# Attention kernel on one core: the weighted sum of values turned around, stationary values in four column groups

## The chip, the cores and the metric

The kernel runs on one core of a Trainium2 chip. The metric is device time in microseconds from launch to end. All arithmetic on data is in f32; the logits use f32r, a form of f32 that TensorE takes in one pass.

## The reference

Two layers, each `x + f(groupnorm(x))`, on an image of 48 channels and 256 x 256 pixels. Layer 0, where the change lies, is attention over patches:

```python
qkv = jnp.einsum('bchw,oc->bohw', x, w_qkv)         # 144 channels
qkv = dwconv3x3(qkv, w_dw)                          # depthwise 3x3
q, k, v = jnp.split(qkv, 3, axis=1)
q, k, v = (heads(q), heads(k), heads(v))            # unfold 4x4 patches with a border of 4: 8 heads, 96 features, 66*66 tokens
q = _l2norm(q); k = _l2norm(k)                      # over the 96 features of a token
attn = jnp.einsum('bhcn,bhcm->bhnm', q, k) * temperature
attn = jax.nn.softmax(attn, axis=-1)                # over m
out = jnp.einsum('bhcn,bhnm->bhcm', v, attn)        # sum over n
out = fold(out.reshape(b, -1, out.shape[-1]), h, w)
out = jnp.einsum('bchw,oc->bohw', out, w_proj)
```

The tokens of the border are zero: their logits are zero, so they only add a constant to each softmax denominator. 4096 tokens of the image remain. Layer 1 multiplies 64 x 64 windows by three sets of matrices along width, height and channels.

## The kernel before, in words

**Stages.** Loading x and its statistics; the pointwise product for heads 0 and 1; the depthwise stage of head 0; attention over eight heads; the projection with the residual and the statistics for layer 1; layer 1. In the profile attention runs from about 288 to 3240 us.

**Attention.** The loop runs over 8 heads, and in each over 16 steps `g` of two blocks of 128 query tokens. The order is written out by hand (`tc.manual_schedule`): each engine gets its instructions in the order of the code. In one step:

- `scores` makes the logits of a block of 128 tokens against all 4096: four times six matmuls (L339) into a PSUM tile of two banks called `big` (three buffers), each followed by an exponential on ScalarE (L574) which writes `e` and its sum. A step makes two such blocks, the second one being the first of the next step.
- `normalised` adds the four sums on VectorE (L587), adds the border's part from a table `e0` made once (L589, `e0` at L563), takes the reciprocal (L591) and scales the block's values with it into `vn` (L593), 128 tokens x 96 features.
- `weigh` makes the weighted sum for all 4096 tokens, in four rounds k. The stationary operand is a piece of `e` of 128 x 64, the moving one is `vn` with 96 columns; two such pieces fill the two column halves of the array. Each round fills 768 columns of a `big` tile (L603), tokens on partitions. VectorE copies it (L612, first step of a head) or adds it (L614) to the sum `oacc` in SBUF.
- Between these, VectorE, ScalarE and POOL do the depthwise convolution of the next head, one row of patches per step in steps 0 to 11: nine taps (L211, L230), squares (L241), their sum (L245), a small matmul `norm` that adds over partitions (L249, `pn`), the inverse square root by three Newton steps on VectorE (`root`, L253 to L270), scaling (L276) and copies and stores to DRAM (L281, L287, L291, L297). The taps of row g-1 and the root of row g-2 are in the same step.
- Head 0 also carries the pointwise product of the other six heads, as strips (L179, L182) between the rounds of `weigh`, in `big` tiles as well.

At the end of a head the sums have tokens on partitions and must have features there. `store` does that for 512 tokens at a time: four transposes on TensorE (L620, `pt` in the PSUM pool `one`), a copy on ScalarE (L623, `oo`) and two DMAs on POOL's queue (L625) to the DRAM tensor `os_`. They are placed behind rounds 1 to 3 of the last step, and the last two in the first step of the next head. POOL's queue also holds the load of key 7 of the next head, ahead of them. SP's queue loads keys, queries, values and rows.

**Behind attention.** The projection loads `os_` (L782, `pot`) in 16 tiles, in pairs: tile t of the upper half of the image and of the lower. A matmul (L796), an addition (L803) and statistics (L807) follow.

Of the kernel before, what the change touches and what calls it, by code (L numbers as in the profile page):

```python
# [1 line left out]

# [6 lines left out]
F32 = mybir.dt.float32  # L9
F32R = mybir.dt.float32r  # L10
AF = mybir.ActivationFunctionType
ALU = mybir.AluOpType
# [10 lines left out]
NH = 8  # L23
HD = C * KK // NH
NT = (H // KS) * (W // KS)
NBORDER = (H // KS + 2) * (W // KS + 2) - NT
# [5 lines left out]
NP1 = CH * HC  # L32
# [7 lines left out]
TP = 256  # L40
# [5 lines left out]
def conv_preact_kernel(  # L46
# [15 lines left out]
    nc = tc.nc  # L62
# [60 lines left out]

    nmul = const.tile([NP1, NH], F32, name="nmul")
    nadd = const.tile([NP1, 1], F32, name="nadd")

    def group_stats(st, mean, rstd, pool, pspool, behind=lambda: None):

# [35 lines left out]
    class Strip:  # L164
# [24 lines left out]
        def store(self):  # L189
            for s, rows in enumerate(both_halves(t1[1], 2 * self.j, 2, base=1)):  # L190
                nc.sync.dma_start(out=rows, in_=self.ot[:, 2 * s : 2 * s + 2, :])

    class Depthwise:
# [57 lines left out]
        def root(self, on_scalar=False):  # L251
            n = self.pool.tile([NP1, PX], F32, name="n", bufs=2)
            nc.vector.tensor_scalar_max(n, self.pn, 1e-24)  # L253
            y = self.pool.tile([NP1, PX], F32, name="y", bufs=2)
            if on_scalar:
                nc.scalar.activation(n, n, AF.Sqrt)
                nc.vector.reciprocal(y, n)
                nc.vector.tensor_scalar(y, y, nmul[:, self.h : self.h + 1], nadd, ALU.mult, ALU.add)
                self.y = y
                return  # L260

            nc.vector.tensor_scalar(
                y.bitcast(mybir.dt.int32), n.bitcast(mybir.dt.int32), -0.5, 1597463007.0, ALU.mult, ALU.add
            )
# [38 lines left out]
    NB = NT // 128  # L303
# [101 lines left out]
    with tc.tile_pool(name="xn", bufs=1) as xnp, tc.tile_pool(name="cst", bufs=1) as cst, tc.tile_pool(  # L405
# [124 lines left out]
    with tc.tile_pool(name="ahead", bufs=2) as ah, tc.tile_pool(name="ae", bufs=3) as ae, tc.tile_pool(  # L530
        name="asm", bufs=6
    ) as asm, tc.tile_pool(name="ao", bufs=1) as ao, tc.tile_pool(name="big", bufs=3, space=PSUM) as big:
        MB = 8
        NK = NB // MB
        NLATE = 1
        RP = TP // PX * KS
        NG = NB // G
        keys, queries, values, oaccs = {}, {}, {}, {}
# [26 lines left out]
        def scores(h, nb):  # L565
# [15 lines left out]
            return h, nb, e, zs  # L581

        def normalised(h, nb, e, zs):

            b = h * NB + nb
# [5 lines left out]
            nc.vector.reciprocal(rz, zu)  # L591
# [4 lines left out]
        def weigh(h, g, blocks, k):  # L596

            ps = big.tile([128, 2, 512], F32, name="big")
            for j in range(MB):
                mb = k * MB + j  # L600
                for i, (e, vn) in enumerate(blocks):
                    for p in (0, 64):
                        nc.tensor.matmul(  # L603
                            ps[p : p + 64, j // 4, j % 4 * HD : (j % 4 + 1) * HD],
                            lhsT=e[:, mb * 128 + p : mb * 128 + p + 64],
                            rhs=vn,
                            start=(i == 0),
                            stop=(i == G - 1),
                        )
            if g == 0:  # L610
                oaccs[h, k] = ao.tile([128, 2, 4 * HD], F32, name="oacc", bufs=5)
                nc.vector.tensor_copy(oaccs[h, k], ps[:, :, : 4 * HD])  # L612
            else:
                nc.vector.tensor_add(oaccs[h, k], ps[:, :, : 4 * HD], oaccs[h, k])  # L614

        def store(h, m):

            pt = one.tile([HD, 4, 128], F32, name="pt", tag="one")
            for i in range(4):
                nc.tensor.transpose(pt[:, i, :], oaccs[h, m // 2][:, m % 2, i * HD : (i + 1) * HD], ident)  # L620
            late = h == NH - 1 and m >= NM - NLATE
            oo = (pe if late else asm).tile([HD, 512], F32, name="oo", bufs=NLATE if late else 2)
            nc.scalar.copy(oo, pt.rearrange("p i n -> p (i n)"))  # L623
            for i in range(512 // TP):
                nc.gpsimd.dma_start(  # L625
                    out=os_[m * (512 // TP) + i, h * HD : (h + 1) * HD, :], in_=oo[:, i * TP : (i + 1) * TP]
                )

        load_query(0, 0)
        for m in range(NM):  # L630
# [13 lines left out]
        with tc.manual_schedule():  # L644
            load_query(0, 1)
            block = scores(0, 0)
            for h in range(NH):
                more = h + 1 < NH
                rows = {r: Depthwise(h + 1, r) for r in range(CR + 1)} if more else {}
                for g in range(NG):  # L650
# [51 lines left out]
                    if g == 0 and h > 0:  # L702
                        for m in range(6, 8):
                            store(h - 1, m)
                    if p:
                        p.patches()
                        p.store((2,))
# [4 lines left out]
                        n.first()  # L712
                    for k in range(NK):
                        s = (h * NG + g) * NK + k
                        weigh(h, g, blocks, k)
                        if k == 0 and d:
                            d.reduce()
                        if k == 0 and p:
                            p.low(nc.gpsimd)
                            p.store((0, 1))  # L720
                        if s % 2:
                            for w in strips[s - 1] + strips[s]:
                                w.run(big.tile([128, 2, 512], F32, name="big"))
# [20 lines left out]
            for m in range(6, 8):  # L744
                store(NH - 1, m)
    attention.close()


# [307 lines left out]
```

## Time and profile before

| | |
|---|---|
| runs | 3646.11, 3650.18, 3638.68 us; median 3646.11 |
| the profiled execution | 3654.33 us, its span 3652.5 us |
| mean granted TensorE clock | 0.974 |
| attention: PE L339, L603 | 6144 and 32768 MATMUL instructions |
| ScalarE L574 | 1024 x 1117 ns, and 1024 x 192 ns to read the sums |
| VectorE L614 | 480 x 954 ns |
| PE L620 and ScalarE L623 | 256 x 277 ns and 64 x 582 ns |

The page gives busy time per engine and the chain of work that ended last. Busy time of PE counts the union of its matmuls, which overlap, so single durations do not add up to it; a price per matmul is read from a stretch of the timeline, as its length over its count. An f32 matmul of the program appears as two MATMUL instructions, an f32r one as one. The span is what the profile covers; the execution's own time is 1.8 us more.

### The profile page before, as it was taken

What the parts mean: (1) busy time and instruction counts of PE and PEld (TensorE: products, weight loads), DVE (VectorE), ACT (ScalarE), POOL (GpSimd) and SP (SyncE); (2) the same over time, 40 slices, a digit from 0 to 9 for tenths busy, and PEclk for the clock granted to TensorE, in tenths of its full rate; (3) what the DMA queues carried; (4) which work ended last, traced back from release to release, by engine and by line L of the source; (5) the groups of instructions that cost most, each with busy time, mean ns of one, the idle gap of its engine ahead of it and who ended that gap; (6) DMA issues with size and microseconds to landing.
All of it is one profiled execution on the core that took longest, in us unless ns stands there. A gap on an engine that the chain in (4) does not pass through costs nothing.

```text
span 3652.5 us, 104961 instructions
## 1 busy us (share of the span) xinstructions
PE 3426.0 (94%) x46578; PEld 2874.1 (79%) x46578; DVE 2115.9 (58%) x3505; ACT 1898.0 (52%) x2699; POOL 531.6 (15%) x616
## 2 busy tenths in 40 slices
PE   2878999999999999999999999999999999976888
PEld 1337777888888888889888888888889888842765
DVE  5464775269727962796289528952894222257454
ACT  0245666566646664665466546654665444410343
POOL 2030121012201220122112111211121100010001
PEclk9988999999999999999999999999999999987899
DMA  7455665533323332333233323332333221059564
GB/s 159 157 125 146 169 183 154 172 92 97 91 74 87 95 86 74 86 93 94 73 82 98 90 81 82 93 86 81 82 93 92 62 54 28 19 141 283 119 156 107
DMA packets 241972, 386.78 MB, mean 106 GB/s; under 512 B 78130, under 2 KB 175778, under 8 KB 237000
## 3 DMA queue, kind: packets, MB, share of 16 engines
q1 hardware_dynamic: 187974, 244.77, 24.0%
q0 software_dynamic: 35264, 106.40, 12.8%
q10 hardware_dynamic: 18274, 28.83, 3.4%
q8 instruction: 368, 6.03, 0.7%
q14 instruction: 92, 0.75, 0.1%
HBM read 234.76 MB, written 144.90 MB: 104 GB/s over the span
## 4 chain that ended last, share of the span: by engine, by line
PE 81%; DMA 4%; DVE 3%; issue 2%; ACT 1%; SPq 1%; ACTq 0%; POOL 0%; POOLq 0%; DVEq 0%
PE big L339 37%; PE big L603 36%; PE pc L961 2%; PE pb L942 2%; PE pa L916 2%; PE big L179 1%; DVE acc L230 1%; PE pt L620 1%; DMA pxt<-in_x_dram 1%; DMA pad<-t 1%; PE pn L249 1%; DMA xs<-in_x_dram 1%; PE pst L557 1%; DVE xt L803 1%; DVE lzt L928 0%
## 5 line engine op out<-in xcount | busy, mean ns | idle before, releaser
L574 ACT ACTIVATE e<-big,nmx 128x1024 f32<-128x1024 f32 x1024 | 1143.9, 1117 | 878.0 <-PE big L339 617.8
L339 PE MATMUL big<-kt,qt 128*128 128x512 f32 x6144 | 1439.9, 393 | 31.9 <-DMA qt<-qkv 21.7
L603 PEld LDWEIGHTS big<-vn,e 128*64 128x64 f32 x32768 | 1358.7, 137 | 57.1 <-ACT e L574 30.6
L603 PE MATMUL big<-vn,e 128*64 128x96 f32 x32768 | 1389.1, 247 | 5.9 <-DVE oacc L614 2.4
L339 PEld LDWEIGHTS big<-kt,qt 128*128 128x128 f32 x6144 | 1148.4, 189 | 279.2 <-issue 29.3
L614 DVE TENSOR_TENSOR oacc<-big,oacc 128x768 f32<-128x768 f32 x480 | 453.4, 954 | 703.7 <-PE big L603 703.7
L230 DVE SCALAR_TENSOR_TENSOR acc<-pad,dwt,acc 126x1024 f32<-126x1024 f32 x592 | 765.6, 1293 | 39.7 <-ACT acc L211 23.9
L587 DVE TENSOR_REDUCE zt<-zs 128x1 f32<-128x4 f32 x256 | 38.5, 150 | 338.7 <-ACT e L574 338.7
L297 POOL DMA_DIRECT2D qkv<-o x72 | 52.8, 734 | 1247.6 <-ACT o L281 1247.6
L291 POOL TENSOR_TENSOR ol<-o,oh 126x1024 fp32r<-126x1024 f32 x78 | 184.7, 2368 | 311.7 <-DVE ss L245 238.4
L574 ACT ACTIVATION_READ_ACCUMULATOR e<-big,nmx 128x1 f32 x1024 | 196.2, 192 | 0.0
L281 ACT COPY o<-acc 126x1024 f32<-126x1024 f32 x74 | 158.8, 2146 | 0.0
L928 DVE COPY lzt<-pa 128x864 f32<-128x864 f32 (+1 forms) x69 | 101.2, 1507 | 69.2 <-PE pa L916 69.2
L949 ACT COPY lyt<-pb 128x1024 f32<-128x1024 f32 x69 | 70.7, 1025 | 116.3 <-PE pb L942 96.9
L241 ACT ACTIVATE sq<-acc 126x1024 f32<-126x1024 f32 x74 | 78.2, 1057 | 101.2 <-DVE acc L230 101.2
L796 PE MATMUL pps<-pot,wp 96*96 96x512 f32 x128 | 77.5, 770 | 56.2 <-DMA pot<-os__70 45.1
L182 ACT ACTIVATE ot<-big,bias 108x1024 f32<-108x1024 f32 x64 | 68.3, 1111 | 113.5 <-PE big L179 76.4
L211 ACT ACTIVATE acc<-pad,dwt 126x1024 f32<-126x1024 f32 x74 | 84.1, 1137 | 81.9 <-DMA pad<-t 81.9
L245 DVE TENSOR_REDUCE ss<-sq 126x64 f32<-126x1024 f32 x80 | 97.5, 1219 | 27.0 <-ACT sq L241 27.0
L942 PEld LDWEIGHTS pb<-wsb,lzt 64*64 64x64 f32 x4608 | 82.2, 140 | 37.2 <-issue 23.4
L219 PE MATMUL dps<-pad,diag 126*126 126x512 f32 x216 | 96.3, 606 | 15.5 <-DMA pad<-t 15.5
L796 PEld LDWEIGHTS pps<-pot,wp 96*96 96x96 f32 x128 | 26.0, 212 | 107.0 <-issue 73.8
(134 smaller groups left out, 2006.8 us busy)
## 6 DMA issues: line engine op xcount, KB each, us to landing
pad<-t SPq DMA_DIRECT2D x238, 254.0 KB
t<-ot SPq DMA_DIRECT2D x128, 217.7 KB
qkv<-ol POOLq DMA_DIRECT2D x78, 336.0 KB, 6.5
qkv<-oh POOLq DMA_DIRECT2D x70, 336.0 KB, 5.7
qt<-qkv SPq DMA_DIRECT2D x176, 96.0 KB
xs<-in_x_dram SPq DMA_DIRECT2D x128, 96.0 KB
os__70<-oo POOLq DMA_DIRECT2D x128, 96.0 KB, 2.1
pot<-os__70 SPq DMA_DIRECT2D x16, 768.0 KB
```

The lines of the kernel that those rows point to most:

```text
L219: nc.tensor.matmul(ps[:, i, :], lhsT=diag[:, tap, :], rhs=self.pad[:, y : y + 2, dx : dx + W], start=(tap == 0), stop=(tap == 8),)
L230: nc.vector.scalar_tensor_tensor(self.acc, self.pad[:, dy : dy + KS, dx : dx + W], dwt[:, self.h, tap : tap + 1], self.acc, ALU.mult, ALU.add,
L245: nc.vector.tensor_reduce(self.ss, self.sq.rearrange("p a (x b) -> p x a b", b=KS), AX.XY, ALU.add)
L281: nc.scalar.copy(self.o.rearrange("p (a b) x -> p a b x", a=KS), self.acc.rearrange("p a (x b) -> p a b x", b=KS))
L291: eng.tensor_sub(self.ol, self.o, self.oh.bitcast(F32))
L339: nc.tensor.matmul(ps[:, i, :], lhsT=qt[:, r, q0 : q0 + 128], rhs=kts[2 * j + i][:, r // 2, :], start=(r == 0), stop=(r == 2),)
L574: nc.scalar.activation(e[:, j * 1024 : (j + 1) * 1024], ps.rearrange("p a b -> p (a b)"), AF.Exp, bias=nmx[:, b : b + 1], accum_out=zs[:, ...
L603: nc.tensor.matmul(ps[p : p + 64, j // 4, j % 4 * HD : (j % 4 + 1) * HD], lhsT=e[:, mb * 128 + p : mb * 128 + p + 64], rhs=vn, start=(i == 0),
L614: nc.vector.tensor_add(oaccs[h, k], ps[:, :, : 4 * HD], oaccs[h, k])
L796: nc.tensor.matmul(ps[:, i : i + step, :], lhsT=wp, rhs=ot[:, ki * KS + i : ki * KS + i + step, part * n : (part + 1) * n], start=True, st ...
L928: nc.vector.tensor_copy(to, src)
L942: nc.tensor.matmul(pb[s * WS : (s + 1) * WS, w, n * WS : (n + 1) * WS], lhsT=zts[u][r, t * C + b * 24 + q * 8 + s * 4 + i, :], rhs=wsb[r, ...
```

## The change

`weigh` swaps its operands. The stationary operand is now a third of `vn`, 128 tokens x 32 features, and the moving one is 512 columns of `e`. Four such pieces stand side by side in four column groups of 32; each writes 32 partitions of a bank of a `big` tile, features on partitions. Three of the groups hold the three thirds for one set of 512 tokens, the fourth holds one third for the last set of four. So eight sets of 512 tokens fill six banks ("slots"), three `big` tiles a step in place of four. `store` then needs no transpose: four DMAs for each pair of slots go from `oacc` to `os_`, right behind the last addition. The fourth pass of the k loop keeps only the strips and loads that were attached to it. The last sum of all has a tile of its own (`last`).

The border's part of the denominator is an exponential with the bias log(NBORDER) into a fifth column of `zs`, at the head of every `scores`; `e0` and L589 go. The small matmul `norm` moves from ahead of `scores` to behind its first six logits. `root` takes one third-order step and one Newton step (seven operations for nine, ten in all), with a constant folded into `nmul3`.

```diff
-            for _ in range(3):
-                nc.vector.tensor_mul(z, y, y)
-                nc.vector.scalar_tensor_tensor(z, z, -0.5, n, ALU.mult, ALU.mult)
-                nc.vector.scalar_tensor_tensor(y, z, 1.5, y, ALU.add, ALU.mult)
-            nc.vector.tensor_scalar(y, y, nmul[:, self.h : self.h + 1], nadd, ALU.mult, ALU.add)
+            nc.vector.tensor_mul(z, y, y)
+            nc.vector.tensor_mul(z, z, n)
+            nc.vector.scalar_tensor_tensor(z, z, -10.0 / 3.0, z, ALU.add, ALU.mult)
+            nc.vector.scalar_tensor_tensor(y, z, 5.0, y, ALU.add, ALU.mult)
+            nc.vector.tensor_mul(z, y, y)
+            nc.vector.scalar_tensor_tensor(z, z, -0.5 * 0.375**2, n, ALU.mult, ALU.mult)
+            nc.vector.scalar_tensor_tensor(y, z, 1.5, y, ALU.add, ALU.mult)
+            nc.vector.tensor_scalar(y, y, nmul3[:, self.h : self.h + 1], nadd, ALU.mult, ALU.add)
...
+        nc.vector.tensor_scalar_mul(nmul3, nmul, 0.375)
...
-        e0 = ao.tile([128, NH * NB], F32, name="e0")
-        nc.scalar.activation(e0, nmx, AF.Exp)
+        border = ao.tile([128, 1], F32, name="border")
+        nc.vector.memset(border, math.log(NBORDER))
...
-            zs = asm.tile([128, 4], F32, name="zs")
+            zs = asm.tile([128, 5], F32, name="zs")
+            nc.scalar.activation(zs[:, 4:5], nmx[:, b : b + 1], AF.Exp, bias=border)
...
+                if j == 0 and behind:
+                    behind()
...
-            zu = asm.tile([128, 1], F32, name="zu")
-            nc.vector.scalar_tensor_tensor(zu, e0[:, b : b + 1], float(NBORDER), zt, ALU.mult, ALU.add)
...
+        def parts_of(slot):
+            q, j = divmod(slot, NS)
+            return q * (NS + 1) + j, q * (NS + 1) + NS, j
...
-            for j in range(MB):
-                mb = k * MB + j
+            for u in range(2):
+                m, last, j = parts_of(2 * pair + u)
                 for i, (e, vn) in enumerate(blocks):
-                    for p in (0, 64):
+                    for p in range(NS + 1):
+                        c, n = (p, m) if p < NS else (j, last)
                         nc.tensor.matmul(
-                            ps[p : p + 64, j // 4, j % 4 * HD : (j % 4 + 1) * HD],
-                            lhsT=e[:, mb * 128 + p : mb * 128 + p + 64],
-                            rhs=vn,
+                            ps[p * 32 : (p + 1) * 32, u, :],
+                            lhsT=vn[:, c * 32 : (c + 1) * 32],
+                            rhs=e[:, n * 512 : (n + 1) * 512],
                             start=(i == 0),
                             stop=(i == G - 1),
                         )
...
+            old = oaccs[h, pair]
+            if h == NH - 1 and g == NG - 1 and pair == 2:
+                oaccs[h, pair] = pe.tile([128, 2, 512], F32, name="last")
+            nc.vector.tensor_add(oaccs[h, pair], ps, old)
...
-            pt = one.tile([HD, 4, 128], F32, name="pt", tag="one")
-            for i in range(4):
-                nc.tensor.transpose(pt[:, i, :], oaccs[h, m // 2][:, m % 2, i * HD : (i + 1) * HD], ident)
...
-            nc.scalar.copy(oo, pt.rearrange("p i n -> p (i n)"))
...
+            for u in range(2):
+                m, last, j = parts_of(2 * pair + u)
+                for p0, p1, n, c in ((0, HD, m, 0), (HD, 128, last, j * 32)):
+                    rows = os_[n * T : (n + 1) * T, h * HD + c : h * HD + c + p1 - p0, :]
+                    nc.gpsimd.dma_start(
+                        out=rows.rearrange("t c n -> c t n"),
+                        in_=oaccs[h, pair][p0:p1, u, :].rearrange("c (t n) -> c t n", t=T),
+                    )
...
                     blocks = [normalised(*block)]
+                    block = scores(h, g * G + 1, p and p.norm)
                     if p:
-                        p.norm()
                         p.root()
-                    block = scores(h, g * G + 1)
...
-                        weigh(h, g, blocks, k)
+                        if k < 3:
+                            weigh(h, g, blocks, k)
+                            if g == NG - 1:
+                                store(h, k)
...
-                        if g == NG - 1 and k > 0:
-                            for m in range(2 * k - 2, 2 * k):
-                                store(h, m)
-            for m in range(6, 8):
-                store(NH - 1, m)
```

More of the change, by code (lines that the diff above doesn't have):

```diff
@@ L1 @@
+import math
 from contextlib import ExitStack
@@ L125, in conv_preact_kernel @@
     nadd = const.tile([NP1, 1], F32, name="nadd")
+    nmul3 = const.tile([NP1, NH], F32, name="nmul3")
     def group_stats(st, mean, rstd, pool, pspool, behind=lambda: None):
@@ L532, in conv_preact_kernel @@
     ) as asm, tc.tile_pool(name="ao", bufs=1) as ao, tc.tile_pool(name="big", bufs=3, space=PSUM) as big:
-        MB = 8
-        NK = NB // MB
-        NLATE = 1
+        NK = 4
+        NS = 3
         RP = TP // PX * KS
@@ L560, in turn, with scores @@
             values[h, m] = vT
-        e0 = ao.tile([128, NH * NB], F32, name="e0")
-        nc.scalar.activation(e0, nmx, AF.Exp)
-        def scores(h, nb):
+        border = ao.tile([128, 1], F32, name="border")
+        nc.vector.memset(border, math.log(NBORDER))
+        def scores(h, nb, behind=None):
             b = h * NB + nb
             e = ae.tile([128, NT], F32, name="e")
-            zs = asm.tile([128, 4], F32, name="zs")
+            zs = asm.tile([128, 5], F32, name="zs")
+            nc.scalar.activation(zs[:, 4:5], nmx[:, b : b + 1], AF.Exp, bias=border)
             kts = [keys[h, m] for m in range(NM)]
@@ L580, in scores @@
                 )
+                if j == 0 and behind:
+                    behind()
             return h, nb, e, zs
         def normalised(h, nb, e, zs):
-            b = h * NB + nb
             zt = asm.tile([128, 1], F32, name="zt")
             nc.vector.tensor_reduce(zt, zs, AX.X, ALU.add)
-            zu = asm.tile([128, 1], F32, name="zu")
-            nc.vector.scalar_tensor_tensor(zu, e0[:, b : b + 1], float(NBORDER), zt, ALU.mult, ALU.add)
             rz = asm.tile([128, 1], F32, name="rz")
-            nc.vector.reciprocal(rz, zu)
+            nc.vector.reciprocal(rz, zt)
             vn = asm.tile([128, HD], F32, name="vn")
@@ L594, in normalised, with weigh @@
             return e, vn
-        def weigh(h, g, blocks, k):
+        def parts_of(slot):
+            q, j = divmod(slot, NS)
+            return q * (NS + 1) + j, q * (NS + 1) + NS, j
+        def weigh(h, g, blocks, pair):
             ps = big.tile([128, 2, 512], F32, name="big")
-            for j in range(MB):
-                mb = k * MB + j
+            for u in range(2):
+                m, last, j = parts_of(2 * pair + u)
                 for i, (e, vn) in enumerate(blocks):
-                    for p in (0, 64):
+                    for p in range(NS + 1):
+                        c, n = (p, m) if p < NS else (j, last)
                         nc.tensor.matmul(
-                            ps[p : p + 64, j // 4, j % 4 * HD : (j % 4 + 1) * HD],
-                            lhsT=e[:, mb * 128 + p : mb * 128 + p + 64],
-                            rhs=vn,
+                            ps[p * 32 : (p + 1) * 32, u, :],
+                            lhsT=vn[:, c * 32 : (c + 1) * 32],
+                            rhs=e[:, n * 512 : (n + 1) * 512],
                             start=(i == 0),
@@ L610, in weigh, with store @@
             if g == 0:
[L611 to L616, printed above, removed]
-            pt = one.tile([HD, 4, 128], F32, name="pt", tag="one")
-            for i in range(4):
[L620 to L627, printed above, removed]
+                oaccs[h, pair] = ao.tile([128, 2, 512], F32, name="oacc", bufs=4)
+                nc.vector.tensor_copy(oaccs[h, pair], ps)
+                return
+            old = oaccs[h, pair]
+            if h == NH - 1 and g == NG - 1 and pair == 2:
+                oaccs[h, pair] = pe.tile([128, 2, 512], F32, name="last")
+            nc.vector.tensor_add(oaccs[h, pair], ps, old)
+        def store(h, pair):
+            T = 512 // TP
+            for u in range(2):
[6 more added lines that the diff above has]
+                    )
         load_query(0, 0)
@@ L701, in conv_preact_kernel @@
                             turn(h + 1, (g - CR - 2) * 2 + m)
-                    if g == 0 and h > 0:
-                        for m in range(6, 8):
-                            store(h - 1, m)
                     if p:
@@ L739, in conv_preact_kernel @@
                                 )
-                        if g == NG - 1 and k > 0:
-                            for m in range(2 * k - 2, 2 * k):
-                                store(h, m)
-            for m in range(6, 8):
-                store(NH - 1, m)
     attention.close()
```

## The prediction, made before the changed kernel was run

> **What bounds the kernel now.** I read the busy shares first, then the chain of waits, then three kinds of detail: the table of windows, the groups, and the timeline of one step.
>
> ```profile
> PE 3426.0 (94%) x46578; PEld 2874.1 (79%) x46578; DVE 2115.9 (58%) x3505; ACT 1898.0 (52%) x2699; POOL 531.6 (15%) x616
> ...
> PE big L339 37%; PE big L603 36%; PE pc L961 2%; PE pb L942 2%; PE pa L916 2%; PE big L179 1%; DVE acc L230 1%; PE pt L620 1%; DMA pxt<-in_x_dram 1%; DMA pad<-t 1%; PE pn L249 1%; DMA xs<-in_x_dram 1%; PE pst L557 1%; DVE xt L803 1%; DVE lzt L928 0%
> ```
>
> TensorE is busy 94% of the span, and the chain that ends last runs 73% through two lines: the logits (L339) and the weighted sum (L603). The table of windows (window, length, then busy us and instructions of PE, PEld, DVE, ACT, POOL, then clock, DMA share, GB/s) says where this is so:
>
> ```profile
> 306.00:745.00 439.00, 429.91 (x5230) 346.78 (x5229) 234.71 (x412) 282.53 (x383) 58.64 (x56) 0.99 0.58 163
> 1103.00:1461.00 358.00, 358.00 (x4951) 321.15 (x4949) 233.42 (x412) 213.35 (x313) 60.69 (x60) 1.00 0.34 86
> 3251.00:3380.00 129.00, 85.56 (x158) 31.10 (x158) 103.65 (x111) 0.41 (x2) 9.09 (x18) 0.74 0.98 272
> ```
>
> From head 1 on PE has no idle time at all: what comes off PE there comes off the span. Head 0 holds 9 us of gaps. The projection stage (3251 to 3380) is a DMA stage, 98% busy, so it moves earlier by as much as its first load does.
>
> The timeline (start, duration, engine, line, count) gives the price of a step, then of a head's boundary, then of the end of attention:
>
> ```profile
> 1505.18 10.78 PE L603 MATMUL big<-vn,e 128*64 128x96 f32 x256
> 1515.89 0.43 PE L249 MATMUL pn<-ss,same 126*126 126x64 f32 x2
> 1516.13 11.15 PE L339 MATMUL big<-kt,qt 128*128 128x512 f32 x48
> 1527.21 10.78 PE L603 MATMUL big<-vn,e 128*64 128x96 f32 x256
> ...
> 1798.90 1.08 PE L620 MATMUL pt<-ident,oacc 128*96 128x128 f32 x8
> 1799.91 2.86 PE L603 MATMUL big<-vn,e 128*64 128x96 f32 x64
> ```
> ```profile
> 3215.28 0.39 PE L603 MATMUL big<-vn,e 128*64 128x96 f32 x4
> ...
> 3237.21 2.03 POOL L625 DMA_DIRECT2D os__70<-oo  x4 [1.14 <-ACT oo L623]
> ...
> 3240.32 21.05 SPq L782 DMA_DIRECT2D pot<-os__70  x7
> ```
>
> A step is 22.03 us (1505.18 to 1527.21), a round of logits and a round of weighted sum of nearly equal length.
>
> **What the Trainium skill says.** "TensorEngine Tiling (Array Packing)", Tiling Modes, lists 128x32 with four tiles that work independently. The trace shows tiles working side by side: a plain f32 matmul of the program is two MATMUL instructions, and the 256 of a step pass in 10.78 us, 0.25 of it the last one's own length, so a pair passes in 10.53/127 = 83 ns. "TensorE: Matmul & The Clock Gate", Part 3, measured 10.6 times for a 4x4 packing of 32x32 tiles. There, four tiles share the same rows, as four column groups over 128 rows do; no line of this trace has more than two tiles on one row. "ScalarE: Activation LUTs", What ACT_TABLE_LOAD costs, gives an ACTIVATE with a pointer bias as 280 ns + 0.833 ns per element: 1133 ns for 1024, where L574 takes 1117.
>
> **The change part by part.**
>
> *Weighted sum on PE.* Before: 128 pairs x 83 ns = 10.6 us a step. After: 3 pairs of slots x 2 x 2 blocks x 4 groups = 48 program matmuls, 96 instructions of 512 columns. If four column groups run together that is 24 rounds. The nearest row is over_h (L961), four tiles of 64x64 (two on a row), also f32 with 512 columns:
>
> ```profile
> 3504.55 2.76 PE L961 MATMUL pc<-lyt,hsb 64*64 64x512 f32 x24
> ```
>
> 24 instructions are six rounds; less the last one's 0.59 (its shortest duration), five intervals take 2.17 us, 0.43 each. So 24 x 0.43 = 10.3 us, 0.3 less, and over 128 steps **-38 us**. The arithmetic that the array does has not shrunk (3 x 4096/4 columns a block against 32 x 96); only the overhead between rounds falls. Both ends: -38 if the four groups overlap fully, and a doubling of the 10.3 if only two do (rival 1).
>
> *Transposes.* Two stores before (8 transposes) put 1.01 us between parts of L603 (1798.90 to 1799.91). Four such pairs per head, 7 boundaries: **-28 us**. The oo copies (L623, 64 x 582 ns) go from ScalarE, where nothing waited at those places but the DMA. 128 store DMAs on POOL's queue at 0.51 us become 96 of the same kind, still behind the load of key 7 and before nothing else of that head; POOL is busy 15%.
>
> *End of attention.* Before, 25.0 us pass from the last step's first L603 (3215.28) to the first pot load (3240.32): the wait for vn, the rounds, then transposes, copies and DMAs in turn. After: resumed 2.1 us in, pairs of slots end at about 4.7, 8.1 and 11.5 us (3.44 each). The first loads need slots of the first two pairs only, and the last pair's sum has its own tile, so their buffers need not wait for it. 8.1 + 0.35 to release + up to 1.8 behind a memset (L760) + 1.23 add + 4 x 0.51 issue + 2.1 landing = 13.8 to 15.6: **-10 us** (-9 to -12). The DMA stage behind it then starts that much earlier.
>
> *Head 0.* The strips between the rounds want `big` buffers that wait for L614, because DVE is still at the taps. One buffer fewer a step and a shorter DVE queue: between 0 and the 9 us of gaps; I take **-4**.
>
> *VectorE, priced at nothing.* Per step: two root operations (2 x 226 ns), two zu (2 x 160) go; four additions of 768 columns at 954 become three of 1024, at the 1225 of L975 (same shape): 3.82 against 3.68. In a depthwise step DVE has some 21.2 us of work in 22.03, so it falls to about 20.2 in 21.7: PE stays the bound and covers it. Without cover, these would have been about 1 us a step. nmul3 is one small operation before attention.
>
> *ScalarE, priced at nothing.* 256 border exponentials, 202 ns (L145, 96x1) to 280 ns (skill) each, 52 to 72 us. The first of a step runs while ScalarE waits for logits (4.6 us there). The second is queued in front of an e, whose logits come every 1.36 us while an e costs 1.31; the lag of 0.2 is below the slack of three `big` buffers. If that cover failed, 72 us would appear. The e0 operation (0.4 us) goes.
>
> *Square sums' matmul moved (norm).* Same 0.2 us of PE, now after the first six logits, 1.4 us later. It issues no DMA. Behind it wait the other 42 logits; its own input was ready before the step. On DVE root follows the addition and normalised, which end 2.2 us into the step; pn is there at about 1.9. So nothing, with an upper end of 0.3 x 70 = 21 us.
>
> Sum: -38 - 28 - 10 - 4 = **-80 us**. Against the profiled execution (3654.3, span 3652.5) 3574; that execution lies 8 us above the median of the runs (3646.1), so for the median **3566 us**.
>
> **Rivals.** (1) *Four column groups over all 128 rows are not fed at full rate* (slower). For: only two tiles per row were ever seen here. Against: the 4x4 figure of the skill. If two pass at once, a round costs 0.86 and the step 10.0 us more: 3646 + 1280 - 42 = 4884. It decides from 80/3072 = 26 ns per round: at 457 ns instead of 430 the whole gain is gone. (2) *ScalarE or the moved matmul becomes visible*: +72, 3638, no measurable change. Against: ACT is 213 of 358 us busy. (3) *The rounds bring nothing* (lead-in of the 32-column groups eats 0.3 us a step), boundaries and end remain: 3604. That the transposes stay is excluded, the code that issues them is gone.
>
> **How the numbers follow.** My forecast 0.71; rival 3 0.10; rival 2 0.04; rival 1 0.15. Only differences above 0.3% (11 us) can be told from no change here. Faster 0.81, same 0.04, slower 0.15. The range takes the forecast with its ends (-38, -28, -12, -9, and 21 back) and rival 3, from 3540 to 3630; rival 1 is left out.
>
> **What would show it.** Right: L603 as some 12288 MATMULs of 128x32 by 512 columns, a round of four every 0.43 us; a plain step of 21.7 us; no L620; the first pot load 10 us sooner after the last scores; PE still without idle from head 1 on. Wrong: rounds above 457 ns, or PE waiting for `e` or for DVE in the steps.

## The result, and the profile after

The changed kernel takes **3595.28 us** (median of 4 runs, 3585.69 to 3602.95) against 3642.40 for the kernel before in the same session: ratio 0.9863, interval [0.9837, 0.9889]. A second set of four runs gave 3604.14 against 3645.51, 0.9879 [0.9862, 0.9896]. So the gain is 41 to 47 us, a little over half of the 80 forecast, inside the range. The profiled execution took 3602.95 (span 3601.1), about 8 above its median, as the one of before was, so the two profiles can be laid side by side.

From the page of the changed kernel, the busy shares (engine, busy us, share, instructions) and the chain that ended last:

```profile
PE 3365.5 (93%) x25842; PEld 1871.5 (52%) x25842; DVE 2026.6 (56%) x2983; ACT 1911.9 (53%) x2890; POOL 523.9 (15%) x584
...
PE big L344 38%; PE big L614 36%; PE pc L968 2%; PE pa L923 2%; PE pb L949 2%; DMA t<-ot 1%; PE big L181 1%; DMA pot<-os__70 1%; DMA vt<-qkv 1%; DMA lxq<-x1s 1%; DVE lzt L935 1%; DMA pad<-t 1%; PE pst L562 1%; DVE xt L810 1%; DMA x1s<-pxt 0%
```

PE still carries the span: logits (now L344) and weighted sum (now L614) make up 74% of the chain. But there are two new names from attention in it that the chain of before did not have: `t<-ot`, the store of a strip, and `vt<-qkv`, a load of values. PE waited for `vt` in head 0 alone, and the strips run in no other head. (L562 is the L557 of before; `pot`, `lxq` and `x1s` belong to the stages behind attention.) The table of windows (window, length, then busy us and instructions of PE, PEld, DVE, ACT, POOL, then clock, DMA share, GB/s), for head 0 and for a stretch of later heads:

```profile
306.00:745.00 439.00, 410.02 (x2516) 210.57 (x2511) 219.54 (x336) 269.07 (x384) 52.58 (x44) 0.96 0.58 156
1103.00:1461.00 358.00, 358.00 (x2398) 202.35 (x2391) 223.37 (x348) 220.03 (x344) 63.85 (x64) 1.00 0.34 88
```

In the later heads PE is busy in every microsecond, as before. In head 0 it now lacks 29 us of the 439, where it lacked 9, and the clock is 0.96 where it was 0.99. The same is seen when the span is cut at the first weighted-sum matmul of the heads and steps (starts from the timeline):

| stretch, us | before | after | difference |
|---|---|---|---|
| start to head 0 | 306.7 | 304.5 | -2.2 |
| head 0 | 438.7 | 460.8 | **+22.1** |
| heads 1 to 6 | 2148.1 | 2100.0 | **-48.1** |
| head 7, up to its last step | 321.8 | 317.7 | -4.1 |
| last step to the first `pot` load | 25.0 | 15.6 | **-9.4** |
| from there to the end | 412.1 | 402.5 | -9.6 |

The last line is no steady effect: in the ten other profiles with the new sum, from the experiments below, this stretch took 403 to 419 us, and 411.3 and 417.5 in the two with the old sum. The four lines ahead of it keep their signs: in the second profile of the changed kernel they read 452.4, 2100.0, 317.7 and 15.6.

Timeline of PE in a depthwise step of the changed kernel, one with the small matmul `norm` (L251); a plain step has none (start, duration, engine, line, operation, output<-inputs, tile size of the array, moving shape, count):

```profile
1486.82 10.51 PE L614 MATMUL big<-e,vn 128*32 128x512 f32 x96
1497.26 1.66 PE L344 MATMUL big<-kt,qt 128*128 128x512 f32 x6
1498.76 0.33 PE L251 MATMUL pn<-ss,same 126*126 126x64 f32 x2
1498.90 9.80 PE L344 MATMUL big<-kt,qt 128*128 128x512 f32 x42
1508.63 10.51 PE L614 MATMUL big<-e,vn 128*32 128x512 f32 x96
```

96 instructions in four column groups pass in 10.51 us. Less the last one's own length (0.59), 23 intervals of a round of four take 9.92 us, 0.43 each: the four groups run together. The step, from one L614 to the next, is 21.81 us against 22.03. A boundary between two heads:

```profile
1772.20 10.51 PE L614 MATMUL big<-e,vn 128*32 128x512 f32 x96
1782.63 11.18 PE L344 MATMUL big<-kt,qt 128*128 128x512 f32 x48
1793.74 8.79 PE L614 MATMUL big<-e,vn 128*32 128x512 f32 x80
```

It is a step like any other now, 21.54 us from 1772.20 to 1793.74; the steps at this place took 25.83 with the transposes. And the end of attention, from the timeline of all engines (SPq is SP's queue of DMA issues; in brackets the idle time before and what ended it):

```profile
3182.94 1.07 PE L614 MATMUL big<-e,vn 128*32 128x512 f32 x8
3185.00 9.65 PE L614 MATMUL big<-e,vn 128*32 128x512 f32 x88 [0.99 <-DVE vn L598]
3194.10 2.33 POOL L637 DMA_DIRECT2D os__70<-oacc  x4 [0.88 <-DVE oacc L628]
3197.32 2.34 POOL L637 DMA_DIRECT2D os__70<-last  x4 [0.89 <-DVE last L628]
3198.59 3.39 SPq L789 DMA_DIRECT2D pot<-os__70  x6
```

15.6 us from the first L614 to the first `pot` load, in time with the stores of the last pair and not behind them.

### The profile page after: what moved, and what is told of

Same layout as the page of the kernel before. It is cut to its first block, busy times and chain, and to the rows that moved or that the text cites. A ratio compares the mean times of both kernels' runs of the same rounds, so it can differ in the third digit from the quotient of the medians.

```text
span 3601.1 us, 63050 instructions
## 1 busy us (share of the span) xinstructions
PE 3365.5 (93%) x25842; PEld 1871.5 (52%) x25842; DVE 2026.6 (56%) x2983; ACT 1911.9 (53%) x2890; POOL 523.9 (15%) x584
## 4 chain that ended last, share of the span: by engine, by line
PE 81%; DMA 6%; DVE 2%; issue 1%; ACT 1%; SPq 1%; ACTq 0%; POOL 0%; POOLq 0%; DVEq 0%
PE big L344 38%; PE big L614 36%; PE pc L968 2%; PE pa L923 2%; PE pb L949 2%; DMA t<-ot 1%; PE big L181 1%; DMA pot<-os__70 1%; DMA vt<-qkv 1%; DMA lxq<-x1s 1%; DVE lzt L935 1%; DMA pad<-t 1%; PE pst L562 1%; DVE xt L810 1%; DMA x1s<-pxt 0%
## 5 line engine op out<-in xcount | busy, mean ns | idle before, releaser
L344 PE MATMUL big<-kt,qt 128*128 128x512 f32 x6144 | 1460.2, 395 | 35.1 <-DMA kt<-qkv 26.8
L614 PE MATMUL big<-e,vn 128*32 128x512 f32 x12288 | 1353.7, 595 | 1.0 <-DVE vn L598 1.0
L344 PEld LDWEIGHTS big<-kt,qt 128*128 128x128 f32 x6144 | 1142.6, 189 | 377.4 <-issue 120.1
L628 DVE TENSOR_TENSOR oacc<-big,oacc 128x1024 f32<-128x1024 f32 x359 | 438.6, 1222 | 784.2 <-PE big L614 784.2
L614 PEld LDWEIGHTS big<-e,vn 128*32 128x32 f32 x12288 | 385.2, 110 | 888.3 <-issue 818.1
L594 DVE TENSOR_REDUCE zt<-zs 128x1 f32<-128x5 f32 x256 | 38.7, 151 | 329.8 <-ACT e L580 329.8
L949 PE MATMUL pb<-wsb,lzt 64*64 64x64 f32 x4608 | 88.8, 223 | 11.4 <-issue 7.2
```

The source lines that it names most:

```text
L344: nc.tensor.matmul(ps[:, i, :], lhsT=qt[:, r, q0 : q0 + 128], rhs=kts[2 * j + i][:, r // 2, :], start=(r == 0), stop=(r == 2),)
L614: nc.tensor.matmul(ps[p * 32 : (p + 1) * 32, u, :], lhsT=vn[:, c * 32 : (c + 1) * 32], rhs=e[:, n * 512 : (n + 1) * 512], start=(i == 0), ...
L628: nc.vector.tensor_add(oaccs[h, pair], ps, old)
L949: nc.tensor.matmul(pb[s * WS : (s + 1) * WS, w, n * WS : (n + 1) * WS], lhsT=zts[u][r, t * C + b * 24 + q * 8 + s * 4 + i, :], rhs=wsb[r, ...
```

## The experiments

The gain of the steps and the head boundaries is there in every profile, so the experiments ask about head 0. My theory was that the change moved **the strips**: a strip (L181 on PE, a copy on ScalarE, a store, then loads on the same queue) runs behind passes 1 and 3 of the k loop. With four rounds these passes were two rounds apart, about 5.3 us. With three, the first pair of strips stands behind two rounds of 3.5 us and the second directly behind the third round, so one round apart, and the next pair is some 11 us of logits and two rounds away. What this runs into was open, and three versions of it were tried: too few buffers (`ot`, `xs`), SP's queue, which issues everything in its written order, or the DMA engines themselves. The rivals were that the added small operations or the moved `norm` cost the time, and, for the steps, that the column groups pass only because of the order in which they are written. Comparisons are with the kernel before on the same chip. Ratios have 95% intervals.

### The changed kernel again

No edit.

> The changed kernel, unaltered, for a second profile and a paired time. Theory A (head 0 suffers because the two pairs of strips are now only one round of the weighted sum apart, 3.6 us instead of 5.3, so SP's queue brings x and carries the results away too late): head 0, from its first weighted sum to that of head 1, takes 455 to 465 us again (438.7 before the change), while heads 1 to 6 take 2100. Rival B (the first profile caught a bad moment of the DMA engines): head 0 takes 430 to 440 this time. Ratio to before 0.985 to 0.989 with A, 0.978 to 0.982 with B.

3604.14 us, 0.9879 [0.9862, 0.9896]. Head 0 took 452.4 us: +13.7 over before, not +22.1. So head 0's loss varies from execution to execution, but it is a loss both times.

### The strips two rounds apart

```diff
-                        if k < 3:
-                            weigh(h, g, blocks, k)
+                        if k != 1:
+                            pair = max(k - 1, 0)
+                            weigh(h, g, blocks, pair)
                             if g == NG - 1:
-                                store(h, k)
+                                store(h, pair)
```

The passes of k that hold strips now come after round 1 and after round 3.

> Only edit: the second and third rounds of the weighted sum come in the passes k = 2 and 3 instead of 1 and 2, so the strips stand between rounds 1 and 2 and behind round 3, two rounds apart (7 us). Theory A: head 0 falls to 425 to 440 us, the total by 20 to 30 us against the changed kernel, ratio to before about 0.979 to 0.981. Rival B: head 0 stays within its scatter, no difference in the medians above 5 us.

3577.45 us, 0.9805 [0.9792, 0.9819]: 27 us below the second set of the changed kernel, taken together with it. Head 0 took **426.1 us** and heads 1 to 6 2100.0, as without the edit. From the windows of the changed kernel and of this one over head 0:

```profile
304.00:765.00 461.00, 432.02 (x2639) 222.72 (x2637) 223.08 (x344) 283.49 (x407) 59.62 (x56) 0.96 0.57 155
```
```profile
303.00:729.00 426.00, 415.60 (x2636) 217.24 (x2636) 223.01 (x344) 284.26 (x406) 59.61 (x56) 1.00 0.59 168
```

The same work, to within three PE instructions, takes 35 us less: PE's idle time goes from 29 to 10 us, and its busy time falls by 16 us, since the clock granted to it is 1.00 on the mean instead of 0.96 (432.0 x 0.96 is 414.7, near the 415.6). The distance of the strips is the cause of head 0's loss. (They are 7.0 us apart here, further than the 5.3 before the change.)

### The new sum alone

The kernel before with only the new `weigh` and `store`; border, roots and `norm` stay as they were.

> The kernel before with the weighted sum and the stores of the change alone: three Newton steps, e0 with its extra VectorE operation, and the matmul norm ahead of the logits stay. If the small parts (roots, border, norm) are hidden as predicted, this is the changed kernel's time within 5 us, a plain step takes 21.5 us and a depthwise step 21.8. Rival C (the small parts pay on the path): it is slower than the changed kernel by 20 us or more, and depthwise steps show PE waiting for DVE, since DVE then has about 21 us of work in 21.8.

3593.01 us, 0.9856 [0.9838, 0.9873]. Head 0 444.2, heads 1 to 6 2097.2, steps of 21.76 and 21.54 us. The whole gain is in this part, and part of the loss in head 0 too: 444.2 where the strips two rounds apart give 428.5 (below). It was expected to take the changed kernel's time within 5 us, and is 11 below its second set; all its runs (3587.5 to 3598.1) lie below all of that set (3598.8 to 3607.3). This suggests, without showing it, that the small parts cost something in head 0 while the strips are close together. Which of them, and how, stays open.

### The small parts alone

The kernel before with the border's exponential, the root in ten operations and the moved `norm`.

> The kernel before with only the small parts: roots in ten operations, the border's exponential on ScalarE, norm behind the first six logits. The weighted sum and the transposes are as before. Prediction: within 5 us of before, steps of 22.03 and 21.81 us unchanged. Rival D (the border's exponentials, 256 of 0.28 us, or the moved matmul appear on the path): slower by up to 72 us. Rival C: faster by 20 us or more.

3650.80 us, 1.0012 [1.0000, 1.0024]. Head 0 437.5 (before 438.7), heads 1 to 6 2150.6 (before 2148.1). Depthwise steps 22.08 us against 22.03, plain ones 21.82 as before. So neither the 256 exponentials nor the roots show; the moved `norm` may cost 0.05 us in each depthwise step.

### One more buffer for the strips

Two kernels, each on the changed one:

```diff
-    NOT = 3
+    NOT = 4
```

and five `xs` buffers in place of three.

> The changed kernel with four ot buffers for the strips' results instead of three (NOT = 4), so that the second pair of strips of a step no longer waits for the DMA that carries off the first. Theory A1 (the wait of ScalarE for that DMA, 20 us in head 0, starts the delay): head 0 falls from 452-461 to below 440 us. Theory A2 (SP's queue is late as a whole, because its work for both pairs falls into one short stretch): ScalarE's wait goes away but head 0 stays above 445, with PE waiting for x (xs) or for values (vt) instead.

> The changed kernel with five xs buffers for the strips' input instead of three, so that SP issues the load of x for the next strips without waiting for TensorE to have read the last ones (SP waits 50 us for that in head 0). Theory A2: SP no longer stands still there, gets ahead, and head 0 falls to 425-440 us, the total by 15 to 25. Theory A1: head 0 stays above 445, since the results' buffers are as scarce as before.

3595.78 us, 0.9865 [0.9835, 0.9895], and 3597.11 us, 0.9857 [0.9820, 0.9894]: neither can be told from the changed kernel. Head 0 took 447.7 and 452.3. Waits over 306 to 745 us (engine, line, what released it, total us, times, longest), in the changed kernel and then with four `ot`:

```profile
ACT ot L184 <- DMA t<-ot: 21.0, 8, 5.2
...
PE pst L562 <- DMA vt<-qkv: 11.6, 5, 4.3
PE big L181 <- DMA xs<-in_x_dram: 11.6, 3, 10.8
...
PE big L344 <- ACT ot L184: 5.8, 3, 2.5
```
```profile
PE pst L562 <- DMA vt<-qkv: 13.9, 5, 3.6
...
ACT ot L184 <- DMA t<-ot: 3.4, 1, 3.4
```

The fourth buffer did what it was to do: ScalarE's wait went from 21.0 to 3.4 us, and PE's wait for ScalarE from 5.8 to 0.5. But that was the smaller part of what PE waits for. Its waits for values (`vt`) and for x (`xs`) were there already, 23.2 us together, or 14.3 in the second profile of the changed kernel, and are 17.7 with four `ot`.

Five `xs` buffers missed what was expected of them if SP's queue is the cause. SP's wait of 50 us for TensorE to have read the old x is gone, but SP waits 60.0 us for ScalarE's results instead, which it has to store in their turn, and so it gets no further ahead.

### The same bunching in the kernel before

```diff
-                        weigh(h, g, blocks, k)
+                        for r in ((0,), (1, 2), (3,), ())[k]:
+                            weigh(h, g, blocks, r)
```

The old sum and all its four rounds, but the strips behind round 3 and round 4, one round apart.

> The kernel before, with the weighted sum as it was, but its rounds 1 and 2 both ahead of the first pair of strips and round 3 ahead of the second, so that the pairs are one round (2.7 us) apart, as after the change. Theory A: head 0 rises from 438.7 to 455-475 us though nothing of the sum has changed, the total by 15 to 35 us. Rival B (head 0's loss comes from the new sum or the longer additions): head 0 stays at 435-442.

3693.80 us, 1.0127 [1.0098, 1.0157]. Head 0 took **479.8 us**, 41 more than before and more than was expected, with nothing of the change in it. Heads 1 to 6 took 2154.8, 6.7 more, because the transposes at the boundaries moved with k (26.96 us there in place of 25.83). Waits over 306 to 745 us in this kernel:

```profile
ACT ot L182 <- DMA t<-ot: 49.6, 12, 7.0
...
PE big L339 <- ACT ot L182: 28.5, 8, 5.0
```

The store of a strip is not done in time, ScalarE waits to write the next one, and PE waits for the `big` tile that ScalarE has not read. So bunched strips cost head 0 time with the old sum too. But this is the smaller of the two waits of the changed kernel, grown large. The larger one is hardly there: PE waits 2.7 us for `xs` and not at all for `vt`. The rounds are shorter here, so that the strips stand 2.7 us apart and not 3.5.

### The row loads on another queue in head 0

```diff
-                            rows[g + 1].load()
+                            rows[g + 1].load((nc.gpsimd,) if h == 0 else (nc.sync,))
```

On the changed kernel, with its strips close together: the loads `pad<-t` of a row of patches go to POOL's queue in head 0, so that SP's queue is shorter. The data moved are the same.

> The changed kernel with the three loads of the next row (pad) of a step of head 0 on POOL's queue instead of SP's. Theory A2 (in head 0 SP's queue, which works through loads for the strips, their stores, the row, values and queries in order, is the late one once its work falls into a shorter stretch): 5.6 to 7.6 us per step leave that queue, PE no longer waits for vt and xs, head 0 falls from 452-461 to 425-440 us, the total by 15 to 30. Rival A3 (the DMA engines themselves, at some 60% load, are late, whichever queue issues): head 0 stays at 445-461.

3580.02 us, 0.9811 [0.9794, 0.9827]. Head 0 took **435.1 us**, with the strips left where the change put them. PE's waits over 306 to 745 us:

```profile
PE big L344 <- ACT ot L184: 12.7, 4, 6.0
...
PE pst L562 <- DMA vt<-qkv: 1.2, 2, 0.6
```

The waits for `vt` and `xs` are all but gone, 1.2 us for 23.2 and 14.3 in the two profiles of the changed kernel. So these come from SP's queue: the same transfers are issued, part of them from a different queue, and the DMA engines as a body had no less to move. Whether the issuing or the order of the transfers within the queue makes them late is not separated, and the edit was not tried on the kernel before, where these two waits are only 3.6 us. The other wait, for ScalarE and its `ot`, is still there. The fourth `ot` and this edit thus each take away one of the two waits; both together were not tried. The larger distance of the strips leaves 3.7 us of the two, besides 6.7 us of waits for VectorE.

SP's waits show the lateness as well, first the changed kernel, then the one with strips two rounds apart, then this one, over 306 to 745 us:

```profile
SPq L318 <- DMA pad<-t: 40.9, 27, 3.1
SPq L318 <- PE big L344: 11.6, 7, 8.8
```
```profile
SPq L318 <- PE big L344: 38.3, 13, 11.4
...
SPq L318 <- DMA pad<-t: 21.5, 17, 2.9
```
```profile
SPq L318 <- PE big L344: 31.0, 12, 7.6
```

L318 is the helper that loads queries, keys and values. A wait of SP for PE's logits means that SP is *ahead*: it stands there with the next query load and waits for the old query to be done with. That was 31 to 38 us in the faster versions (38.5 before the change), and is 11.6 in the changed kernel: SP is *behind*, and has spent the time in waits for its own earlier transfers (40.9 us for `pad`, 27.6 before the change). The timeline of SP's issues around one stall of the changed kernel:

```profile
560.64 12.81 SPq L318 DMA_DIRECT2D qt<-qkv  x12
573.55 2.88 SPq L193 DMA_DIRECT2D t<-ot  x4
576.47 6.32 SPq L175 DMA_DIRECT2D xs<-in_x_dram  x4
```

and PE in the same microseconds:

```profile
570.54 1.97 PE L181 MATMUL big<-xs,wr 48*108 48x512 f32 x8
572.44 3.64 PE L614 MATMUL big<-e,vn 128*32 128x512 f32 x32
586.85 3.90 PE L181 MATMUL big<-xs,wr 48*108 48x512 f32 x8 [10.76 <-DMA xs<-in_x_dram]
```

The strips at L181 want the `xs` loads of 576.47. Those stand on SP's queue behind a query load of 12 issues, which took 12.8 us with its waits, and behind the stores of the last strips. PE stood for 10.8 us. What followed is in the windows behind the stall (586 to 590, 594 and on):

```profile
586.00:590.00 4.00, 3.15 (x8) 1.59 (x8) 0.00 (x0) 0.92 (x1) 0.00 (x0) 0.50 0.59 189
590.00:594.00 4.00, 4.00 (x11) 2.74 (x10) 0.04 (x1) 1.85 (x4) 0.00 (x0) 0.50 0.19 53
594.00:598.00 4.00, 4.00 (x16) 3.21 (x16) 3.65 (x12) 2.62 (x5) 0.00 (x0) 0.85 0.00 0
```

PE came back at a clock of 0.50 and had its full clock again some 8 us later: the eight instructions of L181 took 3.90 us where they took 1.97 before the stall. "TensorE: Matmul & The Clock Gate", What's actually happening, says that an idle window of about 3.4 us halves the clock; the trace agrees with a stall of 10.8 us. It also shows what this sentence does not cover: after a stall of only 2.00 us, from 415.5 on, the clock was 0.50 from 418 to 421. So a stall is paid twice, here with 10.8 us and then with about 4: strips, logits and `norm` from 586.85 to 604.12 took 17.3 us, and the same instructions take 13.3 at full clock (3.54 for the first part from 616.59 on, and 9.73 for the other 42 logits in the step shown above).

### The order of the column groups

```diff
-                for i, (e, vn) in enumerate(blocks):
-                    for p in range(NS + 1):
+                for p in range(NS + 1):
+                    for i, (e, vn) in enumerate(blocks):
```

On the changed kernel: two program matmuls (four instructions) in one column group before the next group's turn, in place of one.

> The changed kernel with the two loops in weigh swapped: both blocks of one column group in a row, then the next group, so that four instructions in a row of the program (two matmuls of two each) go to the same 32 columns. If each column group takes its own instructions as they come, a round of four stays at 0.43 us and a plain step at 21.5. If the order of the program decides what runs side by side, groups overlap less: a step of 26 to 42 us in heads 1 to 7 and a total of 4200 us or more.

One run, 3627.25 us. Head 0 took 459.0, heads 1 to 6 2108.6, 0.09 us more per step. A step's sum in this kernel:

```profile
1487.38 10.58 PE L614 MATMUL big<-e,vn 128*32 128x512 f32 x96
```

10.58 against 10.51 us. The four groups run together in this order as well. The single time is 23 us above the median of the changed kernel's second set. Against that kernel's second profile the steps of heads 1 to 7 explain 10 of them (8.6 and 1.7), head 0 another 7 (459.0 and 452.4), and the stages around attention the rest, which scatter as much from run to run.

### Versions that combine what was learnt

All have the strips two rounds apart. The first also puts `norm` back ahead of `scores`; the second is the new sum alone with the strips spread; the third is the first with four `ot` buffers.

```diff
+                    if p:
+                        p.norm()
+                        p.root()
-                    block = scores(h, g * G + 1, p and p.norm)
-                    if p:
-                        p.root()
+                    block = scores(h, g * G + 1)
```

> The spread strips together with norm back ahead of scores; roots and border as changed. The moved matmul costs 0.05 us a depthwise step by the traces so far (21.81 against 21.76), so heads 1 to 6 fall from 2100 to about 2097, and the total by 3 us against the spread kernel. If the move had hidden a wait of PE for pn, heads 1 to 6 would get longer instead.

> The spread strips and the new sum, with none of the small parts (three Newton steps, e0, norm ahead of scores). If the small parts are worth nothing, equal to the spread kernel with norm back, within 4 us, heads 1 to 6 at 2097. If DVE's extra 1 us per depthwise step matters once the steps are this short, head 0 or heads 1 to 6 are longer by 5 us or more.

> Spread strips, norm back, and four ot buffers. ScalarE still waited 21 us in head 0 of the spread kernel for the DMA that frees an ot; PE waited for ScalarE only 3.7 us there. So at most 4 us less than without the fourth buffer.

| version | median us | ratio | head 0 | heads 1 to 6 |
|---|---|---|---|---|
| strips spread, norm back | 3564.57 | 0.9770 [0.9751, 0.9789] | 429.1 | 2097.2 |
| new sum alone, strips spread | 3571.37 | 0.9781 [0.9764, 0.9798] | 428.5 | 2097.2 |
| strips spread, norm back, four `ot` | 3566.30 | 0.9777 [0.9760, 0.9794] | 427.0 | 2097.2 |

Their intervals overlap: the three cannot be told apart. `norm` put back takes 2.8 us out of heads 1 to 6 (2100.0 to 2097.2), the same amount that it added in the kernel before (+2.5). The first of them has the lowest median of all, 3564.57 us, 83 us below the kernel before (3647.46) on the same chip.

## Why the prediction was right, and where it fell short

**Weighted sum on PE, -38 forecast, -32 found.** The mechanism held: four column groups of 128x32, 24 rounds of 0.43 us, as the row of over_h had given. The size was off. The 0.3 us a step came from rounding: with more digits, the lines of the prediction give 24 x 0.434 = 10.42 and 128 x 82.9 ns = 10.61, 0.2 a step and -25 in all, so the size was not known better than the 6 us by which it missed. The time from the first L614 to the logits behind it is 10.44 us (1486.82 to 1497.26) where before it was 10.71 (1505.18 to 1515.89): 0.27 less, not 0.3. A plain step fell by 0.28 (21.82 to 21.54), a depthwise one by 0.22, the difference being the moved `norm`. Heads 1 to 6 lost 48.1 us, of which 24.1 are six boundaries of 4.01; the other 24.0 over 96 steps are 0.25 a step, 32 over 128. (With the new sum alone, and `norm` not moved, it is 0.28 a step, 36 over 128.) "TensorEngine Tiling (Array Packing)", Key Properties, says that different tiles can execute in parallel, and the trace agrees.

**Transposes, -28: as forecast.** A boundary step took 4.01 us more than a plain one (25.83 and 21.82) and now takes the same.

**End of attention, -10: as forecast**, 9.4. The first `pot` loads went out 15.6 us after the step's first L614, the late end of my 13.8 to 15.6.

**Head 0, -4: the step that failed.** By my own terms head 0 should have lost 13 us: 4 of gaps, 4 of its boundary, 16 steps of 0.3. It grew by 22 us in one profile and by 14 in the other, 35 and 27 above my terms. In the first pair of profiles, whose spans differ by 51 us, that is more than all that is missing from 80. The sum lacks another 6; against that, 12 us came off the start and the stages behind the first `pot` load, where nothing was changed in the work, and that is luck.

I had priced what the strips wait for today, the `big` tile behind L614, and argued that a buffer fewer per step could only help. I had not asked where the strips would stand. The k loop kept four passes with the strips at the odd ones, and three rounds in it, so two pairs of strips came to lie one round apart. With each pair go eight DMAs on SP's queue, four loads and four stores, and they moved too. SP fell behind, PE waited for `xs` and values, ScalarE waited for a free `ot` and PE for ScalarE, and PE then ran at a lower clock. Spreading the strips gives 426.1 us. Bunching them in the kernel before costs 41 us there. Moving the row loads off SP's queue brings most of it back (435.1).

The 426.1 us are 12.6 less than before, as my terms say without this effect, but this agreement is luck in part. PE's idle time is 10 us with the strips spread and was 9 before, so the 4 us of gaps did not come. The boundary and the steps gave 8, and a clock of 1.00 in place of 0.99 about 4 more (an estimate, 1% of 430 us).

What was not settled is how much each kind of DMA on SP's queue contributes, and how the two waits of PE add up. One profile has 461 us and the other 452; in the first, PE stood 10.8 us for `xs` at one place, and its longest stall in the second is 4.0 us. Why is open.

**Small parts at nothing: right for VectorE and ScalarE with the old sum.** The border exponential takes 285 ns in the trace (128x1, groups by shape), the 280 ns that "ScalarE: Activation LUTs", What ACT_TABLE_LOAD costs, gives for a pointer bias, and is hidden: 1.0012 [1.0000, 1.0024] for all the small parts together. The moved `norm` was not quite free. It costs about 0.05 us in each depthwise step, 3 us in heads 1 to 6; I had bounded it at 21 and taken 0. With the new sum and bunched strips, all small parts together may cost up to 11 us (3604.14 and 3593.01); with the strips spread they do not show.

**The rivals.** Rival 1, groups not fed at full rate, is refuted: it needed rounds above 457 ns and they take 430, in either order of the groups. Rival 2, ScalarE or the moved matmul in the way, is refuted at its size of 72 us with the small parts alone. Rival 3, 3604, names nearly the measured time, but for another reason: its mechanism (rounds that bring nothing) did not happen, since every step is shorter. Without the step cuts, the total alone would have seemed to confirm it. The measured times also lie inside the range only through the room that was left for this rival: the ends of my own terms (-38, -28, -9, nothing for head 0, and 21 back) reach to 3592, and 3595 and 3604 were measured. That the range held is luck, for it left no room for the step that failed.

## What to carry to other kernels

When a loop loses an iteration, everything that was hung on its counter moves: draw the new distances of those side tasks, and count the DMAs that each puts on an in-order queue. A buffer on which an engine waits may be only part of the lateness: take it away as a cause, and if the time stays, list what the bounding engine still waits for and look for what those waits share, here one issuing queue. And cut the span at the same instruction in both traces before believing that a total near a rival's number means that rival.

## What the runs showed of the hardware

A stall of PE cost more than its length: 29 us of idle time in head 0, 19 more than with the strips spread, came with another 16 us of slower work, and even a stall of 2.00 us was followed by a clock of 0.50. A queue of DMA issues is a resource of its own: one kind of load on another queue took 17 us off head 0 (452.4 to 435.1) with the transfers unchanged. And column groups do not depend on being written in turn: with two matmuls in a row for each group, a step's 96 instructions took 10.58 us instead of 10.51. "TensorE: Matmul & The Clock Gate", Part 3, describes matmuls as strictly first in, first out in start and end; if that held across the column groups here, instructions that follow each other in one group would each need a round of their own, and 96 could not pass in 24 rounds of 0.43 us, as they do with one matmul or two in a row for each group. The measurement decides: it does not hold between these tiles.
